# Residual and sums on VectorE in the first layer, a Strassen product for the last features, one finish for the last block

## The chip, the cores and the metric

The kernel runs on one core of a Trainium2 chip. The metric is the time on the device in microseconds (us). PE is TensorE, DVE is VectorE, ACT is ScalarE, POOL is GpSimd, SP is SyncE, whose queue issues every DMA. All data are 32-bit floats.

## The reference

There are two layers over 2048 rows (4 x 512) of width 512. Each norms its input, runs a gated feed-forward product of inner width 1376, norms the result and adds it to the input. In the first, the half of each row of gate values that is smallest by size is set to zero.

```python
def _L0_attn_ref(x, w_gate, w_up, w_down):
    s = jax.nn.silu(jnp.einsum('bsh,ih->bsi', x, w_gate))
    ...
    k = int(K_FACTOR * I)                      # 688 of 1376
    _, idx = jax.lax.top_k(-jnp.abs(s), k)
    ...                                        # flat: s as B*S rows
    flat = flat.at[rows, idx.reshape(B * S, k)].set(0.0)
    s = flat.reshape(B, S, I)
    s = s * jnp.einsum('bsh,ih->bsi', x, w_up)
    return jnp.einsum('bsi,hi->bsh', s, w_down)

def _L0_ffn_ref(x, W_gate, W_up, W_down):
    ...
    y = gate * up @ W_down.T                   # gate = silu(xt @ W_gate.T), up = xt @ W_up.T
    return y.reshape(out_shape)

x = x + _layernorm(_L0_attn_ref(_layernorm(x), ...))
x = x + _layernorm(_L0_ffn_ref(_layernorm(x), ...))
```

## The kernel before

**Products.** Most products are formed as 2x2 block products with seven multiplications instead of eight (Strassen in Winograd's form). The class `Seven` runs one: products p1 to p7 go to three PSUM banks, pa, px and py, and `first`, `second` and `third` evict and add up between them. p7 is accumulated onto px only when px has been added to c12, so a product waits for DVE. `stationary_sums` and `moving_sums` make the sums of the operands on the engine that they are given.

**First layer.** Eight `Unit`s of two 128-row tiles. `norm` norms a tile and transposes it into xT; `products` runs the gate products (pg, L404) in three column pieces, evicts them through ACT, makes the sums S (`sums`, on POOL) and the up products (pau, pxu, pyu, L143). `search` looks for each row's threshold in six steps, each two passes of ACT (L456) and a chain of two- and four-element DVE steps (L461 to L481). `turns` transposes the result (ph, L578; evicted by ACT, L582), `down_sums` makes sums for the down projection on DVE, and `finish` calls `downs`; the difference that p3 needs is made on POOL (L620) after p2. Units are staggered: while unit j multiplies, unit j-1 searches, j-2 is turned and j-3 is finished.

**Second layer.** Four `Block`s of four tiles. `pair` makes gate and up for 2 x 128 features at a time, five times, by `Seven`; `down_sums` makes sums on POOL; `rest` makes the last 96 of the 1376 features by plain products (fg, fu, L681); then `finish` calls `downs` for two pairs of tiles. For the first three blocks both pairs go through one call, and the products of the next block lie between; the last block calls `finish` once for each pair.

**Down projection.** `downs` runs p1, p5, p6 for each pair, then p7, p2, p4, p3. Each product loads 640 KB of weights into a `wd` buffer, of which there are three. `rest` in it adds the last 96 features. `out_norm` norms a tile (bn_stats, bn_aggr, the power -0.5 on POOL at L109, scaling at L114), adds the residual xr on POOL (L331), and stores. With `final` it takes the statistics in halves and adds the residual on DVE (L327, L328).

**Order.** The layers are recorded within a block that a scheduler orders by a simulated timeline, engine by engine; what stands in each queue is its choice. Pools decide when a buffer is free: S, wr and w have one buffer, px, pa and py two banks each. The end of the program loads a flag `badi` on every engine (`values_load`, L875) and branches (L876): a second, general path, `layers("g", True)`, runs only if the threshold search failed somewhere. It does not run in the profiled execution. At the start, 18 transposes of the identity run on PE (`warm`).

## Time and profile before

| what | value |
|---|---|
| median of 3 runs | 888.31 us (886.12 to 889.33) |
| the profiled execution, its own time | 887.46 us |
| its span | 885.5 us |
| mean granted clock of PE | 0.993 |
| PE busy | 862.3 us |
| DVE, ACT, POOL busy | 511.8, 300.9, 180.3 us |
| moved by DMA | 117.54 MB |

The profile is of one execution. A matmul of 32-bit floats shows as two records on PE; records overlap, so that a record's duration is longer than the distance to the next. A wait is named by what ended it. The first layer takes about the first half of the span. Windows are us from the span's start.

### The profile page before, as it was taken

To read this page: it belongs to the slowest core of one execution; us is meant where nothing else is said; L and a number is where in the kernel's file an instruction comes from. 1 tells how busy PE (TensorE), PEld (TensorE's weight loads), DVE (VectorE), ACT (ScalarE), POOL (GpSimd) and SP (SyncE) were. 2 spreads that over 40 slices of the span, in tenths; PEclk is the share of its full clock that TensorE was granted. 3 is DMA by queue.
4 is the path that set the end of the run, shared out by engine and by line. 5 is a ranking of instruction groups with operands and counts; after the bars stand their busy time and mean duration, and the time that the engine had idled before them with its cause. 6 is when DMAs were issued, how large, how long until landed. Compare 5 with 4: busy or idle time off the path is not lost. (4 is left out here: it accounts for less than half of the span.)

```text
span 885.5 us, 10211 instructions
## 1 busy us (share of the span) xinstructions
PE 862.3 (97%) x3588; PEld 652.4 (74%) x3588; DVE 511.8 (58%) x1328; ACT 300.9 (34%) x598; POOL 180.3 (20%) x249
## 2 busy tenths in 40 slices
PE   8999999999999899999999999999999999999995
PEld 5656566757667576677788888888788888888784
DVE  4887776775939578766955434554236443444322
ACT  2465575748463757466011111011101112011100
POOL 2120111212212112110433211321203221122221
PEclk9999999999999999999999999999999999999998
DMA  9999413334232343377374003610045002420064
GB/s 317 360 335 345 165 54 119 120 101 143 78 119 98 103 138 102 119 293 262 132 254 150 0 1 113 195 44 0 30 143 167 1 0 65 143 97 1 30 217 156
DMA packets 62924, 117.54 MB, mean 133 GB/s; under 512 B 4816, under 2 KB 36560, under 8 KB 62864
## 3 DMA queue, kind: packets, MB, share of 16 engines
q1 hardware_dynamic: 62864, 116.80, 39.4%
q8 instruction: 30, 0.49, 0.2%
q14 instruction: 30, 0.25, 0.1%
HBM read 97.91 MB, written 18.87 MB: 132 GB/s over the span
## 5 line engine op out<-in xcount | busy, mean ns | idle before, releaser
L456 ACT ACTIVATE ja<-v,cur 128x1376 bf16<-128x1376 f32 x96 | 138.3, 1441 | 76.9 <-DVE cur L481 54.4
L404 PE MATMUL pg<-wg,xT 128*128 128x456 f32 (+1 forms) x384 | 158.0, 559 | 3.4 <-ACT p L408 2.5
L404 PEld LDWEIGHTS pg<-wg,xT 128*128 128x128 f32 x384 | 73.2, 193 | 68.6 <-issue 59.9
L118 POOL TENSOR_TENSOR D<-hTb 128x256 f32<-128x256 f32 x20 | 14.6, 730 | 180.5 <-DVE hTb L672 180.5
L461 DVE TENSOR_SCALAR low<-cur 128x2 int32<-128x2 f32 x48 | 8.7, 181 | 72.0 <-ACT ja L456 72.0
L143 PE MATMUL pau<-wu,xT 128*128 128x344 f32 x128 | 43.6, 452 | 0.0
L143 PE MATMUL pagb<-xTb,wg 128*128 128x256 f32 x160 | 41.4, 379 | 0.0
L143 PE MATMUL paub<-xTb,wu 128*128 128x256 f32 x160 | 41.3, 380 | 0.0
L143 PE MATMUL pxub<-T,wu 128*128 128x256 f32 x160 | 41.2, 380 | 0.0
L143 PE MATMUL pxgb<-T,wg 128*128 128x256 f32 x160 | 41.1, 379 | 0.0
L258 PE MATMUL pad<-wd_p,hT 128*128 128x256 f32 x160 | 39.4, 380 | 1.3 <-DMA wd_p<-in_L_attn_w_down_dram 1.3
L408 ACT ACTIVATE p<-pg 128x456 f32<-128x456 f32 (+1 forms) x48 | 26.0, 544 | 43.1 <-PE pg L404 39.5
L258 PE MATMUL pxdb<-wdb_p,hTb 128*128 128x256 f32 x160 | 36.7, 379 | 2.1 <-DMA wdb_p<-sum_f 2.1
L258 PE MATMUL pxd<-wd_p,hT 128*128 128x256 f32 x160 | 37.2, 380 | 1.5 <-DVE y L293 1.5
L258 PE MATMUL padb<-wdb_p,hTb 128*128 128x256 f32 x160 | 37.1, 379 | 0.9 <-DMA wdb_p<-in_L_ffn_W_down_dram 0.9
L258 PE MATMUL pydb<-wdb_p,D 128*128 128x256 f32 x160 | 37.9, 379 | 0.1
L258 PEld LDWEIGHTS pxd<-wd_p,hT 128*128 128x128 f32 x160 | 30.3, 190 | 7.4 <-DVE y L293 1.7
L258 PEld LDWEIGHTS padb<-wdb_p,hTb 128*128 128x128 f32 x160 | 30.3, 190 | 7.2 <-issue 3.3
L258 PEld LDWEIGHTS pxdb<-wdb_p,hTb 128*128 128x128 f32 x160 | 30.3, 190 | 6.7 <-issue 2.5
L258 PEld LDWEIGHTS pad<-wd_p,hT 128*128 128x128 f32 x160 | 29.6, 190 | 7.4 <-DMA wd_p<-in_L_attn_w_down_dram 1.7
L258 PEld LDWEIGHTS pydb<-wdb_p,D 128*128 128x128 f32 x160 | 30.1, 190 | 6.2 <-issue 2.5
L670 ACT ACTIVATE sg<-sg 128x768 f32<-128x768 f32 x20 | 16.9, 843 | 50.9 <-DVE sg L167 50.9
(221 smaller groups left out, 1721.9 us busy)
## 6 DMA issues: line engine op xcount, KB each, us to landing
wd_p<-sum_a SPq DMA_DIRECT2D x28, 640.0 KB, 4.0
wd_p<-in_L_attn_w_down_dram SPq DMA_DIRECT2D x21, 640.0 KB, 4.2
wdb_p<-sum_f SPq DMA_DIRECT2D x20, 640.0 KB, 4.1
wdb_p<-in_L_ffn_W_down_dram SPq DMA_DIRECT2D x15, 640.0 KB, 4.2
xn<-in_x_dram SPq DMA_DIRECT2D x16, 256.0 KB, 3.1
xr<-in_x_dram SPq DMA_DIRECT2D x16, 256.0 KB, 2.8
x<-y SPq DMA_DIRECT2D x16, 256.0 KB, 2.0
xnb<-x SPq DMA_DIRECT2D x16, 256.0 KB, 3.1
```

Source lines behind the costliest of these rows:

```text
L118: eng.tensor_add(s1, a21, a22)
L143: nc.tensor.matmul(ps, self.left[k][:, c, :], self.right[k][:, c, :], start=first and c == 0, stop=c == 1, skip_group_check=not first,)
L258: nc.tensor.matmul(p[which], p[1](k, c), ws[k][:, c, :], start=first and c == 0, stop=c == HC - 1, skip_group_check=not first,)
L404: nc.tensor.matmul(pg, self.xT[:, i, c, :], wg[:, c, c0:c1], start=(c == 0), stop=(c == NH - 1),)
L408: nc.scalar.activation(p[:, c0:c1], pg, AF.Silu)
L456: nc.scalar.activation(junk, v, AF.Sign, bias=cur[:, 0, i : i + 1], accum_out=cur[:, 1, i : i + 1],)
L461: nc.vector.tensor_scalar(low, cur[:, 1, :], 0.0, None, ALU.is_gt)
L670: nc.scalar.activation(sg[:, 1:, :], sg[:, 1:, :], AF.Silu)
```

## The change

- `Unit.sums` and the difference for p3 in the first layer are made by DVE instead of POOL.
- `out_norm` has three forms: for the first layer (`dst is x1`) the mean is subtracted and the residual added in one more DVE step; in the second layer it is as before, but for the very last tile, which is normed straight from PSUM (`pa`).
- In the turns of the last but one unit, DVE evicts every second tile instead of ACT.
- `Block.rest` becomes one product by `Seven`: gate and up stand as the two block rows, so its stationary sums are made once, on DVE, ahead of the blocks.
- In `downs` the addition of px to y moves from p2 to p7. The last block finishes both pairs in one call, in the order p7, p3, then p4 and p2 of the first pair, p4 and p2 of the second.
- At the start the first piece of wg is loaded ahead of the second x tile, and six transposes of the first normed tile are added.
- `values_load` and the branch are now within the scheduled block.

```diff
@@ -95,12 +95,13 @@
     def bank(tag, nm):
         return psum.tile([P, 512], F32, tag=tag, name=nm)
 
-    def moments(src, nm, kind, n=1):
-
+    def moments(parts, nm, kind):
+
+        n = len(parts)
         bufs = 1 if kind == "f" else 5
         st = small.tile([P, n, 6], F32, tag="st" + kind, name=f"st_{nm}", bufs=bufs)
-        for i in range(n):
-            nc.vector.bn_stats(st[:, i, :], src[:, ts(i, H // n)])
+        for i in reversed(range(n)):
+            nc.vector.bn_stats(st[:, i, :], parts[i])
         mv = small.tile([P, 2], F32, tag="mv" + kind, name=f"mv_{nm}", bufs=bufs)
         nc.vector.bn_aggr(mv, st)
         ve = small.tile([P, 1], F32, tag="ve" + kind, name=f"ve_{nm}", bufs=bufs)
@@ -110,7 +111,7 @@
         return mv, rs
 
     def layernorm(dst, src, nm, kind):
-        mv, rs = moments(src, nm, kind)
+        mv, rs = moments([src], nm, kind)
         nc.vector.tensor_scalar(dst, src, mv[:, 0:1], rs, ALU.subtract, ALU.mult)
 
     def stationary_sums(eng, a11, a12, a21, a22, s1, s2, s4):
@@ -135,8 +136,8 @@
         def __init__(self, nm, left, right, c12, c21, c22):
             self.left, self.right = left, right
             self.c12, self.c21, self.c22 = c12, c21, c22
-            n = c12.shape[-1]
-            self.pa, self.px, self.py = [bank(k, f"{k}{nm}")[:, :n] for k in ("pa", "px", "py")]
+            m, n = c12.shape
+            self.pa, self.px, self.py = [bank(k, f"{k}{nm}")[:m, :n] for k in ("pa", "px", "py")]
 
         def product(self, ps, k, first=False):
             for c in range(2):
...
@@ -248,12 +250,12 @@
             ]
             st.append((tiles, left, last, pa, px, py, ya, yb))
 
-        def product(k, which, i=None):
+        def product(k, which, i=None, part=slice(None)):
 
             if k not in ws:
                 ws[k] = down_right(work, key, k, w_d, f"{nm}_{pairs[0][0][0]}")
             first = i is not None
-            for p in [st[i]] if first else st:
+            for p in [st[i]] if first else st[part]:
                 for c in range(HC):
                     nc.tensor.matmul(
                         p[which], p[1](k, c), ws[k][:, c, :],
@@ -282,48 +284,78 @@
         def p7():
             product("p7", PX)
             for p in st:
+                tiles, left, last, pa, px, py, ya, yb = p
+                nc.vector.tensor_add(yb[:, hi], yb[:, lo], px)
                 pz.append(bank("pt", f"pz{nm}_{p[0][0]}")[:, :H2])
                 rest(pz[-1], p, 1, hi, True)
 
-        def p2():
-            product("p2", PA)
+        def c22():
             for p, z in zip(st, pz):
                 tiles, left, last, pa, px, py, ya, yb = p
-                rest(pa, p, 0, lo)
-                nc.vector.tensor_add(yb[:, hi], yb[:, lo], px)
                 nc.vector.tensor_add(yb[:, hi], yb[:, hi], py)
                 nc.vector.tensor_add(yb[:, hi], yb[:, hi], z)
-                nc.scalar.copy(ya[:, lo], pa)
-
-        def p4():
-            product("p4", PX)
-            for p in st:
+
+        def p2(part=slice(None)):
+            product("p2", PA, None, part)
+            for p in st[part]:
+                tiles, left, last, pa, px, py, ya, yb = p
+                rest(pa, p, 0, lo)
+                if not final:
+                    nc.scalar.copy(ya[:, lo], pa)
+            if not final:
+                c22()
+            else:
+                for p in st[part]:
+                    tiles, left, last, pa, px, py, ya, yb = p
+                    if p is st[-1]:
+                        out_norm(work, tiles[0], ya, res, dst, nm, pa)
+                    else:
+                        nc.scalar.copy(ya[:, lo], pa)
+                        out_norm(work, tiles[0], ya, res, dst, nm)
+
+        def p4(part=slice(None)):
+            product("p4", PX, None, part)
+            for p in st[part]:
                 tiles, left, last, pa, px, py, ya, yb = p
                 rest(px, p, 1, lo)
                 nc.vector.tensor_add(yb[:, lo], yb[:, lo], px)
                 out_norm(work, tiles[1], yb, res, dst, nm)
 
-        def p3():
-            product("p3", PY)
-            for p in st:
+        def p3(part=slice(None)):
+            product("p3", PY, None, part)
+            for p in st[part]:
                 tiles, left, last, pa, px, py, ya, yb = p
                 rest(py, p, 0, hi)
                 nc.vector.tensor_add(ya[:, hi], ya[:, hi], py)
-                out_norm(work, tiles[0], ya, res, dst, nm, final)
+                if not final:
+                    out_norm(work, tiles[0], ya, res, dst, nm)
 
         heads = [
             f
             for i in range(len(pairs))
             for f in (lambda i=i: p1(i), lambda i=i: product("p5", PY, i), lambda i=i: p6(i))
         ]
-        return heads + [p7, p2, p4, p3]
-
-    def out_norm(work, t, y, res, dst, nm, final=False):
+        if not final:
+            return heads + [p7, p2, p4, p3]
+
+        ends = [lambda f=f, i=i: f(slice(i, i + 1)) for i in range(len(pairs)) for f in (p4, p2)]
+        return heads + [p7, c22, p3] + ends
+
+    def out_norm(work, t, y, res, dst, nm, pa=None):
+
 
         xr = work.tile([P, H], F32, tag="xr", name=f"xr{nm}_{t}")
         nc.sync.dma_start(xr, res[ts(t, P), :])
-        if final:
-            mv, rs = moments(y, f"o{nm}_{t}", "f", 2)
+        if pa is not None:
+            parts = [pa, y[:, H2:]]
+            mv, rs = moments(parts, f"o{nm}_{t}", "f")
+            for i in range(2):
+                nc.vector.tensor_scalar(
+                    y[:, ts(i, H2)], parts[i], mv[:, 0:1], None, ALU.subtract
+                )
+            nc.vector.scalar_tensor_tensor(y, y, rs, xr, ALU.mult, ALU.add)
+        elif dst is x1:
+            mv, rs = moments([y], f"o{nm}_{t}", "o")
             nc.vector.tensor_scalar(y, y, mv[:, 0:1], None, ALU.subtract)
             nc.vector.scalar_tensor_tensor(y, y, rs, xr, ALU.mult, ALU.add)
         else:
@@ -375,7 +407,7 @@
             s = self.work.tile([P, 3, 2, P], F32, tag="S", name=f"S{self.nm}_{self.j}", bufs=1)
             a, b = self.xT[:, 0], self.xT[:, 1]
             self.left = stationary_sums(
-                nc.gpsimd, a[:, :2], a[:, 2:], b[:, :2], b[:, 2:], s[:, 0], s[:, 1], s[:, 2]
+                nc.vector, a[:, :2], a[:, 2:], b[:, :2], b[:, 2:], s[:, 0], s[:, 1], s[:, 2]
             )
 
         def products(self, wg, right, gate_fill, up_fill):
@@ -579,9 +611,10 @@
                         pt[: isz[i], c, :], h[:, i * P : i * P + isz[i]], ident
                     )
                 nf = n if g0 + n <= FULL else n - 1
-                nc.scalar.copy(hT[:, g0 : g0 + nf, :], pt[:, :nf, :])
+                copy = nc.vector.tensor_copy if other and k else nc.scalar.copy
+                copy(hT[:, g0 : g0 + nf, :], pt[:, :nf, :])
                 if nf < n:
-                    nc.scalar.copy(end, pt[: isz[-1], nf, :])
+                    copy(end, pt[: isz[-1], nf, :])
 
             return [lambda k=k, g0=g0: turn(k, g0) for k in range(2) for g0 in range(0, NI, 4)]
 
@@ -617,7 +650,7 @@
             steps[-3]()
             for u in units:
                 a12, s2 = u.dleft["p3"], u.dleft["p6"]
-                nc.gpsimd.tensor_sub(a12, a12, s2)
+                nc.vector.tensor_sub(a12, a12, s2)
 
         return steps[:-3] + [p2] + steps[-2:]
 
@@ -671,20 +704,21 @@
             ms[1].third()
             nc.vector.tensor_mul(h[:, 1:, :], sg[:, 1:, :], h[:, 1:, :])
 
-        def rest(self, wg, wu):
+        def rest(self, left):
 
             n = I - 2 * HF
             nm = f"{self.nm}_{self.b}"
-            pg, pu = bank("pa", f"fg{nm}"), bank("px", f"fu{nm}")
-            for ps, w in ((pg, wg), (pu, wu)):
-                for c in range(NH):
-                    nc.tensor.matmul(
-                        ps[:n, :], w[:, c, 2 * HF :], self.xT[c // 2][:, c % 2, :],
-                        start=(c == 0), stop=(c == NH - 1),
-                    )
+            t = self.work.tile([P, 4, N2], F32, tag="w", name=f"sgr{nm}", bufs=1)[:n]
+            m = Seven(f"rb{nm}", left, self.right, t[:, 0, :], t[:, 1, :], t[:, 2, :])
+            m.first()
+            c11 = m.second()
             h = self.big.tile([P, N], F32, tag="b5", name=f"hTb{nm}_r")
-            nc.scalar.activation(h[:n, :], pg[:n, :], AF.Silu)
-            nc.vector.tensor_mul(h[:n, :], h[:n, :], pu[:n, :])
+            lo, hi = h[:n, :N2], h[:n, N2:]
+            nc.scalar.activation(lo, c11, AF.Silu)
+            m.third()
+            nc.scalar.activation(hi, m.c12, AF.Silu)
+            nc.vector.tensor_mul(lo, lo, m.c21)
+            nc.vector.tensor_mul(hi, hi, m.c22)
             self.h.append(h)
 
         def down_sums(self, c):
@@ -742,8 +776,12 @@
             units = [Unit(j, nm, big, work) for j in range(NU)]
             units[0].load(0)
             units[0].norm(0)
+            if not general:
+                for i in range(6):
+                    nc.tensor.transpose(warm[:, i % 4, :], units[0].x[0][:, :P], ident)
+            wg = load_weight(wpool, a_wg, "wg", f"1{nm}", CH[:1])
             units[0].load(1)
-            wg = load_weight(wpool, a_wg, "wg", f"1{nm}", CH)
+            load_weight(wpool, a_wg, wg, f"1{nm}", CH[1:])
             units[1].load(0)
             units[1].load(1)
             wu = load_weight(
@@ -853,28 +891,31 @@
                 for f in finish([units[-1]], wr):
                     f()
             wr = last_rows(f_wd, 2)
+            t = work.tile([P, 3, 2, I - 2 * HF], F32, tag="S", name=f"wrs{nm}", bufs=1)
+            rest = stationary_sums(
+                nc.vector,
+                *[w[:, 2 * c : 2 * c + 2, 2 * HF :] for w in ws for c in range(2)],
+                t[:, 0], t[:, 1], t[:, 2],
+            )
             for b, block in enumerate(blocks):
                 last = b + 1 == len(blocks)
                 for a in range(HC):
                     block.pair(a, lefts)
                     block.down_sums(a)
-                block.rest(*ws)
-                if last:
-                    block.finish([0], wr)
-                    block.finish([1], wr, True)
-                else:
+                block.rest(rest)
+                if not last:
                     for k in range(TB):
                         blocks[b + 1].norm(k)
                     blocks[b + 1].sums()
-                    block.finish([0, 1], wr)
+                block.finish([0, 1], wr, last)
 
         return badi
 
     with tc.block(schedule_with_timeline_sim=True):
         badi = layers("", False)
-    nbad = nc.values_load(badi[0:1, 0:1], min_val=0, max_val=2 * P * NTT)
-    with tc.If(nbad > 0):
-        layers("g", True)
+        nbad = nc.values_load(badi[0:1, 0:1], min_val=0, max_val=2 * P * NTT)
+        with tc.If(nbad > 0, label="general"):
+            layers("g", True)
 
 
 # ---- launch: one core; inputs and outputs as the reference has them ----
```

## The prediction

> **What bounds the kernel now.** I read the page's busy shares and slices first, then the list of waits of PE, then windows cut on the clock's own borders, then the timeline around each wait of PE.
>
> ```profile
> PE 862.3 (97%) x3588; PEld 652.4 (74%) x3588; DVE 511.8 (58%) x1328; ACT 300.9 (34%) x598; POOL 180.3 (20%) x249
> DVE  4887776775939578766955434554236443444322
> PEclk9999999999999999999999999999999999999998
> ```
>
> PE is busy for 862.3 of 885.5 us. Time can come only from fewer columns streamed through PE, from its 23 us of idle time, or from stretches at half clock. DVE is half empty in the second layer (right half of its digits) and well filled in the first.
>
> ```profile
> PE pg L404 <- ACT p L408: 2.5, 1, 2.5
> PE pxdb L258 <- DMA wdb_p<-sum_f: 2.1, 1, 2.1
> PE pxd L258 <- DVE y L293: 1.5, 1, 1.5
> PE ph L578 <- ACT hT L582: 1.4, 2, 1.1
> PE pad L258 <- DMA wd_p<-in_L_attn_w_down_dram: 1.3, 1, 1.3
> PE padb L258 <- DMA wdb_p<-in_L_ffn_W_down_dram: 0.9, 1, 0.9
> ```
>
> The waits are few and single: two belong to the last block's weight loads (wdb_p), the rest to the first layer and the passage to the second.
>
> ```profile
> 5.30:8.70 3.40, 1.69 (x12) 1.03 (x10) 1.09 (x2) 1.29 (x4) 1.28 (x3) 1.00 1.03 388
> 8.70:12.10 3.40, 3.40 (x5) 1.66 (x6) 0.00 (x0) 0.00 (x0) 1.95 (x3) 0.50 1.04 400
> 295.40:298.80 3.40, 1.24 (x3) 0.68 (x4) 0.58 (x2) 3.27 (x5) 0.55 (x1) 1.00 0.00 0
> 298.80:302.20 3.40, 3.40 (x6) 1.62 (x5) 3.10 (x10) 2.24 (x9) 0.10 (x1) 0.51 0.00 0
> 862.05:865.47 3.42, 2.13 (x10) 1.52 (x8) 0.42 (x1) 0.00 (x0) 0.01 (x1) 1.00 0.93 272
> ```
>
> Columns after the length: busy us of PE, PEld, DVE, ACT, POOL, then the granted clock. A stretch of 3.4 us in which PE is busy for 1.69 or 1.24 us is followed by one at half clock; 2.13 us (third kind) is not punished: the clock stayed at 1.00 behind it. Half clock over 3.4 us costs 1.7 us, twice in this execution.
>
> ```profile
> 285.57 1.27 POOL L331 TENSOR_TENSOR y<-y,xr 128x512 f32<-128x512 f32 x1 [2.10 <-issue]
> 285.77 1.08 DVE L477 SCALAR_TENSOR_TENSOR r<-r,d 128x2 f32<-128x2 f32 x1
> 295.53 1.44 ACT L456 ACTIVATE ja<-v,cur 128x1376 bf16<-128x1376 f32 x1 [3.20 <-DVE cur L481]
> 297.56 2.99 PE L404 MATMUL pg<-wg,xT 128*128 128x464 f32 x5 [2.48 <-ACT p L408]
> ```
>
> A two-element DVE step of the threshold search, 0.15 us elsewhere, takes 1.08 us and ends with POOL's addition. The search is late, ACT stands in line for `cur`, the eviction of pg stands behind it, PE waits 2.48 us and then runs at half clock.
>
> ```profile
> 866.33 2.40 PE L258 MATMUL pxdb<-wdb_p,hTb 128*128 128x256 f32 x10 [2.15 <-DMA wdb_p<-sum_f]
> 876.22 0.60 PE L264 MATMUL pydb<-wr,hTb_r 96*128 96x256 f32 x2
> 876.79 1.26 POOL L331 TENSOR_TENSOR yb<-yb,xrb 128x512 f32<-128x512 f32 x1 [0.66 <-DVE yb L114]
> 879.00 0.75 DVE L328 SCALAR_TENSOR_TENSOR yb<-yb,rs_ob,xrb 128x512 f32<-128x512 f32 x1 [0.44 <-POOL rs_ob L109]
> ...
> L875 SPq TENSOR_LOAD <-badi x1: 520/520/520, 880.2 to 880.2; - x1
> L876 SPq COMPARE_BRANCH  x1: 45/45/45, 881.1 to 881.1; - x1
> L876 SPq EVENT_SEMAPHORE  x8: 17/17/17, 883.6 to 884.2; - x8
> ```
>
> PE ends at 876.82 (call it T). The last DVE step starts at T+2.18, SP issues the store until 880.15, loads badi, branches at 881.1 and goes on at 883.6: 8.7 us without PE.
>
> **The change part by part.** The profiled execution took 887.46 us (span 885.5), 0.85 below the median 888.31 of the runs; the sum is made against 887.46.
>
> *The last 96 features (`Block.rest`).* Pace first: four 512-column records take 1.88 us, of which one is 0.592 long, so 0.429 each; ten 256-column ones take 2.32 with 0.379, so 0.216. Before: 64 records of fg and fu over 4 blocks, 16 x 0.429 = 6.86 us a block. After: 7 products x 2 halves x 2 records = 28 x 0.216 = 6.04. Weight loads of 96 columns take 0.163, under the pace. Gain 0.82 x 4 = 3.3 us. The new evictions (DVE about 2.2 us more a block) fall where DVE is at 4 tenths; the new dependences (p7 behind an addition to px) lie, in the built order, behind 6 or more matmuls of 0.43 us of the following down projection. Its own preparation is four DVE sums, about 1.2 us, at the passage.
>
> *One finish for both pairs of the last block.* Seven loads of 640 KB fewer, and each serves twice the matmuls. Before, PE's waits there are 0.94, 2.15 and 0.45 us, with the restart (0.1 each) 3.7. After, with three wd buffers: p7's load starts when p1 is through and has 14 matmuls of 0.43 us or more, 6.0 us, against 4.1 to land. p3's and p4's start together when p5 is through; p4 is wanted 12 matmuls (5.2 us) later, but lands second: 4.2 us plus 655 KB at the 400 GB/s of the window rows (1.6) is 5.8. I charge 0.8 us of new waiting (bounds 0 and 1.5). Net -2.9.
>
> *The end.* In the built order p4 and p2 of pair 1 come last. p2's own chain loses the addition to y (0.46 us with its gap). But p4's chain (addition 0.42, statistics 0.69, 0.18, 0.15, rs 0.55, scaling 0.55, with gaps 2.8) must fit into p2's 2.6 us, and starts late behind pair 0's: it ends near T+0.4. Then POOL adds its residual for 1.27 us, and the last rs (0.55) is queued behind that addition: about T+1.7 to T+2.3, final step at T+2.35 instead of 2.18. The last xr load is queued on SP behind a store that waits for POOL and lands near T+2.3: no better. Against it, SP's badi load and check stand far ahead in the queue, so its branch follows the store at once: 881.1-880.15 = 0.95 us, capped by the landing of the store and by DVE, which left its branch at 882.8: I take 0.9. Net -0.7. At its new place the badi load waits for a DVE step that precedes by several matmuls those that the loads queued behind it wait for: priced at nothing; its cover is that wait for PE; without it every us would delay a down weight of the last unit.
>
> *The start.* wg's first piece is issued ahead of the second x tile: 256 KB less before it, 0.7 us at 388 GB/s, and PE's 0.92 us wait before 8.63 was on it: -0.7 (xT allows no more). The second x tile lands later, at about 8.5, and is normed under four matmuls. The six added transposes fill that hole. *The rule weighed here:* the Trainium skill ("TensorE: Matmul & The Clock Gate", Part 4: PE-mode transpose) says that transposes do not count as PE activity for the clock; by it the six are worth nothing. The rows speak otherwise: up to 5.3 us PE had run only transposes (18, at half pace), and from 5.30 the clock is 1.00. With them the stretch 5.3 to 8.7 has about 0.3+1.2+0.8 = 2.3 us of PE work, above the unpunished 2.13. By the rows -1.7 us, by the rule 0; I take the rows, and keep 0 for the range since the stretches need not lie alike in every execution.
>
> *First layer: work from POOL to DVE.* Onto DVE: 32 sums of 128x256 (from the 128x512 row 0.684 and the 128x688 row 0.87: 0.41 each) 13.1; 8 differences of 128x640 at 0.82, 6.6; 16 residuals, each 0.48 (L327) + 0.75 (L328) for 0.55 (L114), 11.0; some turned tiles copied, 1.9: 33 us. Off POOL: 29.1 (S sums) + 12.3 (L620) + 20.4 (L331) = 62 us. POOL and DVE hold each other up, as the timeline shows (1.08 for 0.15 above). Means beside the undisturbed lines of the timeline: L463 226 ns against 170 (48 of them), L470 215 against 160, L477 205 and L473 203 against 150 (40 each), L513 389 against 150 (8), L491 1703 against 1650 (16): about 12 us of DVE's time is such waiting. So DVE's net is about +21 us on some 320 busy in 440. DVE at 80% does not bound by itself; the cover is PE's backlog. What the lock caused, the 2.48 us wait with its 1.7 us of half clock and the 1.5 us on y L293 (a 0.55 us scaling took 1.75 there), can go: 5.7 us. The y addition also moves from p2 to p7. Bounds: -8, every such wait gone, to +5, new waits on a fuller in-order DVE, among them residual steps that wait for xr or rs with the search queued behind. I take -2.0. The ACT wait (1.4) and the wd_p wait (1.3) stay: loads and order there are the same.
>
> Sum: -3.3 -2.9 -0.7 -0.7 -1.7 -2.0 = -11.3: 876.2 for a like execution, 877.0 beside the median.
>
> **The rivals.** *Only the certain parts:* the clock gives nothing at the start and the first layer nets to nothing or +2: -7.6 to -5.6, 881 to 883. For it: scheduling against a model leaves a few waits in any order. *All locks gone:* -8 in the first layer, 871. *Slower: DVE becomes the bound of the first layer.* Place: search and passage, where DVE is 19.89 us busy of 20 (420 to 440) and gets some 5 us more. Price: each us of the 33 that PE's backlog doesn't cover. 11 us uncovered undo the gain, 16 make it slower by 0.5%; half uncovered gives 893. Against it: before, PE waited only about 2.5 us for DVE in that layer. *It doesn't do what it says:* the six transposes may end before the hole does, or p4's load be late by more; both are inside the first rival.
>
> **How the numbers follow.** Forecast 874 to 880: 0.50. Certain parts only: 0.27. All locks gone: 0.08. DVE bound: 0.15, half of it slower. A change of about 0.5% (4.4 us) can be told from none here. Faster by more: 0.50+0.08, 0.22 of the second, 0.03 of the last = 0.83; within: 0.10; slower: 0.07. The range 870.5 to 884 leaves out the DVE case and the edges.
>
> **What would show it.** Right: two 256-column record groups in place of fg and fu; no wait of PE on wdb_p over 1 us; PEclk 1.00 from 8.7 us on; SP's branch within 0.1 us of the last store; fewer search steps over 0.5 us. Wrong: PE waits for DVE by more than 10 us before 450 us, or a clock still at 0.50 after the start; a final DVE step later than T+3 would make the end a loss.

## The result, and the profile after

The changed kernel takes 874.58 us (median of 6 runs, 872.70 to 877.11) against 887.16 us of the kernel before beside it (6 runs, 885.12 to 889.33): ratio 0.9863, 95% interval 0.9846 to 0.9880. The forecast was 877.0 (870.5 to 884.0). The profiled execution of after took 873.69 us with a span of 871.9: 13.8 us less than the one of before, where the sum had 11.3.

The page of after, busy times and two rows of the slices:

```profile
PE 855.0 (98%) x3642; PEld 659.8 (76%) x3642; DVE 526.8 (60%) x1417; ACT 302.8 (35%) x601; POOL 117.7 (14%) x193
DVE  5887787776939587667956444454346442444424
PEclk9999999999999999999999999999999999999998
```

PE is busy 7.3 us less, and idle 6.3 us less; it fills 98% of the span. DVE's digits in the first layer are hardly higher than before, although POOL has lost 62.6 us. The clock's digits are 9 up to the last slice.

PE's waits (total, times, longest):

```profile
PE pxub L144 <- DVE hTb L160: 1.8, 1, 1.8
PE ptb L376 <- DVE badi L889: 0.9, 1, 0.9
PE pad L260 <- DMA wd_p<-in_L_attn_w_down_dram: 0.9, 1, 0.9
PE pxu L144 <- DVE c L154: 0.9, 1, 0.9
PE ph L610 <- ACT xTb L378: 0.3, 1, 0.3
```

No wait on wdb_p is left, none on y and none of weight on ACT's p. The two longest that are new (hTb, badi) lie in the passage to the second layer.

The windows at the start and around the longest wait (length; busy us of PE, PEld, DVE, ACT, POOL; granted clock; share and rate of DMA):

```profile
3.40:6.82 3.42, 3.26 (x16) 2.86 (x15) 1.58 (x4) 0.00 (x0) 0.55 (x1) 1.00 1.03 389
6.82:10.23 3.41, 3.41 (x15) 2.06 (x14) 1.58 (x4) 0.65 (x2) 0.55 (x1) 1.00 1.05 397
...
467.62:471.03 3.41, 1.58 (x8) 1.08 (x7) 1.53 (x5) 0.37 (x1) 0.31 (x1) 1.00 0.08 31
471.03:474.44 3.41, 3.41 (x18) 2.93 (x16) 2.14 (x4) 0.00 (x0) 0.23 (x1) 1.00 0.00 0
```

In the stretch ahead of pg's first product PE is busy for 3.26 of 3.42 us, and no half clock follows. (The 1.00 of this first row is no reading. The transposes in it start 0.21 us apart up to 6.67 us and 0.11 us apart from 6.86 on: the clock was at half until about 6.82, where the trace's first record of it begins.) At 467.62 PE is busy for only 1.58 of 3.41 us, and yet the clock stays at 1.00; more on that below.

The wait on hTb, from the timeline:

```profile
465.17 0.40 SPq L368 DMA_DIRECT2D xnb<-x  x1
469.11 0.69 DVE L104 BATCH_NORM_STATS2 st_ib<-xnb 128x6 f32<-128x512 f32 x1 [4.24 <-DMA xnb<-x]
469.72 0.40 DVE L160 TENSOR_TENSOR hTb<-hTb,pxub 128x256 f32<-128x256 f32 x1
470.17 1.13 PE L144 MATMUL pxub<-T,wu 128*128 128x256 f32 x4 [1.83 <-DVE hTb L160]
```

The statistics of a tile of the third block (st_ib) stand on DVE ahead of the step that PE needs (L160). DVE waits 4.24 us for the tile's load, issued at 465.17 and landed at 469.08, and PE waits 1.83 us for DVE.

The search steps on DVE, in groups; first two of before, then the same two of after:

```profile
L463 DVE COPY_PREDICATED lo<-low,cur 128x4 f32<-128x4 int32 x48 | 10.9, 226 | 1.0
L477 DVE SCALAR_TENSOR_TENSOR r<-r,d 128x2 f32<-128x2 f32 x40 | 8.2, 205 | 0.9
...
L495 DVE COPY_PREDICATED lo<-low,cur 128x4 f32<-128x4 int32 x48 | 7.7, 160 | 0.8
L509 DVE SCALAR_TENSOR_TENSOR r<-r,d 128x2 f32<-128x2 f32 x40 | 6.2, 155 | 0.8
```

L495 is L463 of before, and L509 is L477, which was 205 ns in the mean and took 1080 ns in one instance, at 285.77 us. Now they run at 155 to 160 ns. DVE's busy time up to the flag's matmul is 328.2 us for 325.2, although POOL's there fell from 84.1 to 25.1.

The end, from the timeline of DVE, POOL and SP; then the rows of the branch by its source line (DVE and SP: branch, and the semaphore instructions behind it, with first and last start):

```profile
859.41 0.42 SPq L348 DMA_DIRECT2D xrb<-x  x1
...
862.21 0.55 DVE L115 TENSOR_SCALAR yb<-yb,mv_ob,rs_ob 128x512 f32<-128x512 f32 x1 [0.66 <-POOL rs_ob L110]
863.83 1.43 DVE L353 TENSOR_SCALAR yb<-yb,mv_ob 128x256 f32<-128x256 f32 x1
863.85 1.26 POOL L363 TENSOR_TENSOR yb<-yb,xrb 128x512 f32<-128x512 f32 x1 [1.68 <-DMA xrb<-x]
865.07 0.60 POOL L110 TENSOR_TENSOR rs_ob<-ve_ob,nhalf 128x1 f32<-128x1 f32 x1
865.13 1.68 SPq L364 DMA_DIRECT2D out_dram<-yb  x2
865.70 0.75 DVE L356 SCALAR_TENSOR_TENSOR yb<-yb,rs_ob,xrb 128x512 f32<-128x512 f32 x1 [0.44 <-POOL rs_ob L110]
```

```profile
L917 DVEq COMPARE_BRANCH  x1: 76/76/76, 866.6 to 866.6; - x1
L917 SPq COMPARE_BRANCH  x1: 45/45/45, 866.9 to 866.9; - x1
L917 DVEq EVENT_SEMAPHORE  x1: 21/21/21, 870.3 to 870.3; - x1
L917 SPq EVENT_SEMAPHORE  x8: 17/17/17, 870.0 to 870.5; - x8
```

PE's last product ends at T = 862.42. POOL waits 1.68 us for the xrb issued at 859.41, adds for 1.26 us, and only then makes the last rs. DVE's subtraction beside that addition takes 1.43 us (0.34 in e8, where no addition runs beside it). The last DVE step starts at T + 3.28; before it was T + 2.18.

Where the 13.6 us of span went, by marks that every kernel here has: the flag's matmul (pbad), the first pagb product of the second block, the first product of the last block's last 96 features, PE's end, the span's end. All times in us; the medians were each taken beside runs of the kernel before, whose median was 885.8 to 887.7.

| kernel | start to flag | to second block | to last block's last features | to PE's end | to span's end | median, ratio to before (interval) |
|---|---|---|---|---|---|---|
| before | 448.24 | 118.06 | 262.46 | 48.05 | 8.69 | |
| after | 437.48 | 120.47 | 261.11 | 43.35 | 9.49 | 874.58, 0.9863 (0.9846 to 0.9880) |
| e1, three moves undone | 447.64 | 119.46 | 261.17 | 43.46 | 11.67 | 886.73, 1.0002 (0.9989 to 1.0015) |
| e2, before with the moves | 439.04 | 122.93 | 262.98 | 48.10 | 9.05 | 882.46, 0.9952 (0.9936 to 0.9968) |
| e3, no transposes | 436.13 | 123.77 | 261.10 | 43.56 | 9.63 | 875.41, 0.9869 (0.9845 to 0.9892) |
| e4, end and ACT's queue | 438.10 | 118.91 | 261.15 | 43.67 | 8.27 | 872.91, 0.9850 (0.9827 to 0.9873) |
| e5, residual on POOL | 440.22 | 118.15 | 261.19 | 43.35 | 10.59 | 877.64, 0.9903 (0.9884 to 0.9922) |
| e6, plain features | 436.39 | 123.41 | 262.46 | 44.18 | 10.66 | 876.58, 0.9886 (0.9868 to 0.9904) |
| e7, two finishes | 436.27 | 121.97 | 261.23 | 46.89 | 8.35 | 876.85, 0.9899 (0.9881 to 0.9916) |
| e8, end and c buffers | 436.29 | 119.80 | 261.13 | 43.35 | 8.43 | 870.43, 0.9818 (0.9804 to 0.9833) |
| e9, e8 and flag on ACT | 438.41 | 118.39 | 261.50 | 43.75 | 8.25 | 873.08, 0.9844 (0.9816 to 0.9872) |
| e10, before with the start | 453.60 | 118.08 | 262.46 | 47.80 | 8.86 | 892.34, 1.0065 (1.0042 to 1.0087) |
| e11, flag's load outside | 436.31 | 121.08 | 261.21 | 43.35 | 12.35 | 876.28, 0.9886 (0.9857 to 0.9916) |
| e12, e2 and the start | 438.89 | 122.08 | 262.46 | 48.11 | 8.96 | 882.35, 0.9944 (0.9924 to 0.9965) |

Half clock is in these figures, 1.7 us for each stretch: two in before's first column, two in e3's second and one in that of e2, e6, e7, e8, e11 and e12; after has none from 6.82 us on. So 3.4 of the 10.8 us that after gains up to the flag are half clock of the one execution of before. After and e8, whose products stand in the same order up to the flag, differ by 1.2 us there: less than that can't be read from one trace.

From before to after: -10.8 to the flag, +2.4 in the passage, -1.35 and -4.7 in the rest of the second layer, +0.8 at the end.

### The profile page after: what moved, and what is told of

The parts are those of the page before. It is cut to its first block, busy times and chain, and to the rows that moved or that the text cites. A ratio compares the mean times of both kernels' runs of the same rounds, so it can differ in the third digit from the quotient of the medians.

```text
span 871.9 us, 10340 instructions
## 1 busy us (share of the span) xinstructions
PE 855.0 (98%) x3642; PEld 659.8 (76%) x3642; DVE 526.8 (60%) x1417; ACT 302.8 (35%) x601; POOL 117.7 (14%) x193
## 5 line engine op out<-in xcount | busy, mean ns | idle before, releaser
L436 PE MATMUL pg<-wg,xT 128*128 128x456 f32 (+1 forms) x384 | 154.8, 549 | 0.2 <-ACT p L440 0.2
L119 POOL TENSOR_TENSOR D<-hTb 128x256 f32<-128x256 f32 x20 | 14.6, 729 | 169.7 <-DVE hTb L705 169.7
L110 POOL TENSOR_TENSOR rs_o<-ve_o,nhalf 128x1 f32<-128x1 f32 x16 | 11.6, 724 | 188.6 <-DVE ve_o L108 188.5
L144 PEld LDWEIGHTS pxub<-T,wu 128*128 128x128 f32 x160 | 30.1, 190 | 6.9 <-DVE hTb L160 2.2
```

The lines of the kernel that those rows point to most:

```text
L110: nc.gpsimd.tensor_tensor(rs, ve, nhalf, ALU.pow)
L119: eng.tensor_add(s1, a21, a22)
L144: nc.tensor.matmul(ps, self.left[k][:, c, :], self.right[k][:, c, :], start=first and c == 0, stop=c == 1, skip_group_check=not first,)
L436: nc.tensor.matmul(pg, self.xT[:, i, c, :], wg[:, c, c0:c1], start=(c == 0), stop=(c == NH - 1),)
```

## The experiments

**e1: the three moves undone.**

```diff
-                nc.vector, a[:, :2], a[:, 2:], b[:, :2], b[:, 2:], s[:, 0], s[:, 1], s[:, 2]
+                nc.gpsimd, a[:, :2], a[:, 2:], b[:, :2], b[:, 2:], s[:, 0], s[:, 1], s[:, 2]
...
-                nc.vector.tensor_sub(a12, a12, s2)
+                nc.gpsimd.tensor_sub(a12, a12, s2)
...
-        elif dst is x1:
+        elif False:
```

> The changed kernel, but in the first layer the residual addition, the sums S and the fourth down operand's difference are made by POOL again; all else stays as changed. Theory A (locks): what the first layer gained came from taking POOL's work out of DVE's way. Then DVE steps over their undisturbed length come back (19.5 us before the flag's matmul in the kernel before, 0.0 in the changed one), PE waits on ACT or DVE again before 450 us, and the run is 4 to 6 us longer than the changed kernel (875): 879 to 881. Rival B (order): the gain came from the earlier addition of px, the turned tiles on DVE and the luck of the schedule; then the time stays within 1.5 us of 875 though the long DVE steps are back. In both the wait of PE on hTb at the passage (2.2 us of distance) should shrink if the residual on DVE causes it, and stay if the late load of xnb alone does.

886.73 us: the whole gain is gone, twice what theory A had asked for. 10.2 us of it are lost ahead of the flag. One of the waits, from the timeline of e1:

```profile
351.81 0.72 POOL L119 TENSOR_TENSOR S<-xT 128x256 f32<-128x256 f32 x1 [4.52 <-issue]
351.90 0.65 DVE L505 SCALAR_TENSOR_TENSOR r<-lo,r 128x2 f32<-128x2 f32 x1
352.61 0.73 POOL L120 TENSOR_TENSOR S<-S,xT 128x256 f32<-128x256 f32 x1
352.78 0.57 DVE L513 TENSOR_TENSOR cur<-lo,r 128x2 f32<-128x2 f32 x1
353.41 0.73 POOL L122 TENSOR_TENSOR S<-xT,S 128x256 f32<-128x256 f32 x1
353.45 1.44 ACT L488 ACTIVATE ja<-v,cur 128x1376 bf16<-128x1376 f32 x1 [1.77 <-DVE cur L513]
...
354.89 0.54 ACT L440 ACTIVATE p<-pg 128x464 f32<-128x464 f32 x1
...
355.48 1.04 PE L436 MATMUL pg<-wg,xT 128*128 128x464 f32 x2 [1.52 <-ACT p L440]
```

POOL's sums S (L119, L120, L122) run beside two search steps of two elements, which take 0.65 and 0.57 us for the usual 0.16 (the Trainium skill, "SBUF — State Buffer", section "Who interferes with whom", has DVE and GpSimd share a pair of ports under an exclusive lock; these rows agree); ACT stands idle 1.77 us ahead of the search's pass, 0.9 of which are what the two steps took too long; the eviction of pg stands behind it, and PE waits 1.52 us. A gap beyond PE's pace is the distance between the starts of two records less the usual one for their shape. Between 100 us and the flag e1 has 11 gaps of over 0.3 us beyond the pace (behind ACT's p, c, xT, he and hT, and DVE's c, D, ve_o and y), 11.1 us in all, where after has two, 0.8 us: the difference is about the 10.2 us. DVE steps that run longer than their kind usually does add up to 21.6 us ahead of 450 us in e1, 32 steps, each beside an instruction of POOL, and to none in after. The chain is that of the prediction, its size is not. But the scheduler orders each kernel anew (one in six of PE's records up to the flag stands elsewhere in e1), and how much of the 10.2 us is the new order and how much the stretched steps is not shown. The wait on hTb in the passage is gone in e1, the one on badi (1.7 us) is there.

**e2: the three moves alone, on the kernel before.** The same three edits.

> The kernel before, with nothing changed but these three moves from POOL to DVE in the first layer. Theory A (locks): 4 to 6 us shorter than the kernel before (887): 881 to 883; the flag's matmul comes about 7 us earlier, the passage costs some 2 to 3 us of it. Rival B (order): 885 to 889, no difference to be told. Rival C, the one of the prediction that ends slower (DVE as the bound): over 889.

882.46 us, 3.6 less than before (886.01). The flag comes 9.2 us earlier, 3.4 of which are the two stretches at half clock of the trace before that this one does not have. The passage then takes 4.9 us more than before. The waits of e2, and the windows at its passage:

```profile
PE pxub L143 <- DVE hTb L159: 1.9, 1, 1.9
PE pz L264 <- DVE badi L855: 1.8, 1, 1.8
```

```profile
468.80:472.21 3.41, 1.55 (x8) 1.05 (x6) 1.53 (x5) 0.37 (x1) 0.00 (x0) 1.00 0.22 83
472.21:475.62 3.41, 3.41 (x10) 2.69 (x9) 0.91 (x2) 0.00 (x0) 0.55 (x1) 0.50 0.00 0
...
4.59:8.00 3.41, 1.97 (x14) 1.29 (x12) 1.83 (x7) 0.74 (x3) 1.17 (x2) 1.00 0.93 306
8.00:11.41 3.41, 2.54 (x7) 1.37 (x8) 1.27 (x3) 0.56 (x2) 0.00 (x0) 1.00 1.03 395
```

1.9 and 1.8 us of waits stand where before had none, and the one on hTb is followed by 3.4 us at half clock (1.7 us). So the moves are worth 5.8 us up to the flag here, with the half clock of before taken out, and 10.2 in e1, where neither trace has any; what is left of it at the end depends on the passage.

**e3: without the six transposes.**

```diff
             if not general:
-                for i in range(6):
-                    nc.tensor.transpose(warm[:, i % 4, :], units[0].x[0][:, :P], ident)
+                pass
```

> The changed kernel without the six added transposes at the start; the order of the loads stays. By the rows of the trace of before (a stretch with little PE work is followed by one at half clock): the hole of 0.8 us ahead of 7.5 us comes back, and one stretch of 3.4 us is granted half clock: +1.7 us against the changed kernel, and the clock of the first 14 us shows 0.50 once. If the six only fill a hole that the clock does not punish: within 0.3 us, clock 1.00 throughout. By the rule that transposes do not count for the clock: 0 as well.

875.41 us, no difference from after that can be told. pg starts at 7.51 us as in after, the clock is full from 6.99 us to 440 us, and the flag is even earlier. So the six are worth nothing that can be told, and the 1.7 us that were expected of the rows did not come. The clock of this execution does fall twice in the passage, which after's did not:

```profile
467.79:471.20 3.41, 1.38 (x7) 0.88 (x7) 1.53 (x5) 0.37 (x1) 0.21 (x1) 1.00 0.02 9
471.20:474.61 3.41, 3.41 (x10) 2.69 (x9) 0.88 (x2) 0.00 (x0) 0.34 (x1) 0.50 0.00 0
437.07:440.48 3.41, 1.70 (x9) 1.01 (x9) 3.02 (x10) 0.00 (x0) 0.77 (x2) 1.00 0.96 314
440.48:443.89 3.41, 3.41 (x9) 2.70 (x9) 1.80 (x3) 0.00 (x0) 1.01 (x1) 0.50 0.82 301
```

From the product ahead of the wait on hTb to the next are 2.4 us here, and 2.2 in after, with the clock's borders at 467.79 instead of 467.62.

**e4: the end and the passage mended, first try.** Within the last block the residual tiles of the last pair are loaded at c22 into xn buffers, the last residual but one is added by DVE, and xn of the second layer is loaded through ACT's queue.

```diff
+            if final:
+                for t in st[-1][0]:
+                    xrs[t] = residual(work, t, res, nm, "xn", bufs=3)
...
-        elif dst is x1:
+        elif dst is x1 or dve:
...
-            normed_T(load_x(self.work, x1, t, nm), t, dsts, nm)
+            normed_T(load_x(self.work, x1, t, nm, eng=nc.scalar), t, dsts, nm)
```

> The changed kernel with two mends. At the end: the last pair's residual tiles are loaded when p7 is through, into the free xn buffers, and the last residual but one is added by DVE instead of POOL, so that nothing stands on POOL ahead of the last rs. At the passage: the second layer's input tiles are loaded through ACT's queue instead of SP's, so that they do not stand behind stores that wait for a residual. If the end is as read in the trace (POOL waits 1.68 us for xrb, adds for 1.26, the last rs stands behind it), the last DVE step starts at PE's end + 2.4 instead of + 3.28: -0.9 us. If the wait on hTb comes from xnb standing behind a store, it goes: -2 us more, 872 in all. Rival: ACT's own queue holds the loads as long, or ACT is held by them: the passage stays at its 2.2 us or grows.

872.91 us. The end took 8.27 us for 9.49, as expected. In the passage this wait of PE fell from 1.8 to 1.1 us and did not go: through ACT's queue the load is issued at 464.32 for 465.17, so SP's queue was not all that held it: the transposes that free an xn buffer start at 463.80 and take 0.49 us.

**e5: only the residual back on POOL.**

```diff
-        elif dst is x1:
+        elif False:
```

> The changed kernel, but in the first layer only the residual addition is back on POOL; the sums S and the difference stay on DVE. With all three back on POOL the flag's matmul came 10.2 us later (447.64 for 437.48). If the harm goes by POOL's time, the residual is 20.4 of its 62 us: a third, flag near 441, and 3 to 4 us longer in all: 878. If the residual is the harmful one (1.27 us long and on the path of a tile's norm, while the sums are four short steps of 0.45 us): most of the 10, 883 or more. If the long POOL chain of the sums S is the one: within 1 us of the changed kernel. For the passage: from the flag to the second block the changed kernel takes 120.5 us, 2.4 more than the kernel before although its last features are 0.8 shorter; if the residual step on DVE causes that, it falls to 118; if the early statistics of xnb do, it stays at 120.

877.64 us, 3.1 above after. The flag is 2.7 us later, a quarter of e1's 10.2, so that sums S and the difference have by far the most (7.4, by the difference between the two runs; it was not run alone). In e5 ten DVE steps are stretched, by 8.7 us, and PE's gaps up to the flag are 3.2 us. The passage is 2.3 us shorter than after's: with the residual on POOL the order there is another, and the wait on hTb is not there.

**e6: the last 96 features by plain products.** `rest` and its call as in the kernel before.

```diff
-                block.rest(rest)
+                block.rest(*ws)
```

> The changed kernel, but with the last 96 features by plain products as in the kernel before. By the pace of records: +0.82 us a block, +3.3 in all (878), of it +2.5 between the second block's first product and PE's end (304.5 in the changed kernel), and no new wait. Rival: the dependences of the seven products cost part of it, and the plain form loses less than 2 us.

876.58 us, 2.0 above after, with intervals that overlap. The trace tells more: from the second block's first product to PE's end 306.64 for 304.46, 2.2 us for three blocks instead of the 2.5 of the sum. The end is longer in e6 as the last xrb landed late:

```profile
871.00 0.75 DVE L356 SCALAR_TENSOR_TENSOR yb<-yb,rs_ob,xrb 128x512 f32<-128x512 f32 x1 [2.83 <-DMA xrb<-x]
```

**e7: the last block in two calls.**

```diff
-                block.finish([0, 1], wr, last)
+                if last:
+                    block.finish([0], wr)
+                    block.finish([1], wr, True)
+                else:
+                    block.finish([0, 1], wr)
```

> The changed kernel, but the last block finishes its two pairs of tiles in two calls, so that each of the seven weights is loaded twice. By the waits of the kernel before: +3.7 us of PE's waits on wdb_p, in two or three waits of 0.5 to 2.2 us, from the last features of the last block to PE's end (43.35 us in the changed kernel, so 47). Rival: the new order of products (p3 ahead of p4 and p2) asks for the loads early enough, and it costs under 1 us. The end after PE's last record may move by half a us either way.

876.85 us. To PE's end 46.89 us for 43.35: +3.5. The waits are back on the doubled loads, and one on DVE's turn at the bank:

```profile
PE pxdb L260 <- DMA wdb_p<-sum_f: 1.5, 2, 1.2
PE pydb L260 <- DVE yb L295: 1.0, 1, 1.0
```

**e8: the end mended, and other buffers at the passage.** The end as in e4, loads on SP, and

```diff
-            normed_T(load_x(self.work, x1, t, nm), t, dsts, nm)
+            kw = dict(tag="c", bufs=2) if self.b > 1 else {}
+            normed_T(load_x(self.work, x1, t, nm, **kw), t, dsts, nm)
```

> The changed kernel with the end mended as before (the last pair's residual tiles loaded when p7 is through, the last residual but one on DVE), and the loads left on SP's queue; at the passage the third and fourth blocks' input tiles use the buffers of c, which the second layer leaves free. The load of the third block's first tile at 465 us waits for an xn buffer (freed by the transposes that end at 464.0), and its statistics stand on DVE ahead of the step that PE waits for. If that buffer is the cause, the wait on hTb at 468 to 470 goes: -2 us, and with the end -3, 871.5. Rival: the statistics, standing earlier on DVE, wait for the same 4 us load at an earlier place and hold other steps: no gain at the passage or a loss of up to 3 us.

870.43 us, ratio 0.9818 (0.9804 to 0.9833): faster than both kernels, 4.1 us below after. The wait on hTb is gone and the end takes 8.43 us:

```profile
PE ptb L388 <- DVE badi L902: 1.7, 1, 1.7
PE pad L260 <- DMA wd_p<-in_L_attn_w_down_dram: 0.3, 1, 0.3
```

```profile
862.14 0.61 POOL L110 TENSOR_TENSOR rs_ob<-ve_ob,nhalf 128x1 f32<-128x1 f32 x1 [1.64 <-DVE ve_ob L108]
862.82 0.75 DVE L368 SCALAR_TENSOR_TENSOR yb<-yb,rs_ob,xrb 128x512 f32<-128x512 f32 x1
```

The last rs follows its ve at once, and the last DVE step starts 2.25 us after PE's end (860.57) instead of 3.28. The 1.7 us for badi that are left are followed by a stretch at half clock in this execution.

**e9: e8, and the flag evicted by ACT.**

```diff
-                nc.vector.tensor_copy(badi, pb[:1, :1])
+                nc.scalar.copy(badi, pb[:1, :1])
```

> The last one (end mended, third and fourth block's input tiles in the buffers of c) with one more edit: the flag badi is evicted by ACT instead of DVE. In that one PE waits 1.9 us at 438 us for the bank of pbad, because DVE's eviction stands behind statistics that wait for a load of xnb, and the stretch after it is granted half clock (440.9). If that is the cause, the wait goes, and with it 1.7 us of half clock wherever the clock's borders had punished it: 2 to 3.5 us less than 870.4, so 867 to 868.5. Rival: PE only waits a little later for the same statistics (the transposes of xnb come next on PE), and nothing or 0.5 us is won.

873.08 us: no better, by the medians worse. The rival held: the wait on badi is gone, and 1.3 us for ve_ib stand in its place. PE also waited in this execution at 36 and 71 us, for the norm of xn and for c, 2.6 us beyond its pace.

**e10: the new start alone, on the kernel before.**

```diff
-            units[0].load(1)
-            wg = load_weight(wpool, a_wg, "wg", f"1{nm}", CH)
+            if not general:
+                for i in range(6):
+                    nc.tensor.transpose(warm[:, i % 4, :], units[0].x[0][:, :P], ident)
+            wg = load_weight(wpool, a_wg, "wg", f"1{nm}", CH[:1])
+            units[0].load(1)
+            load_weight(wpool, a_wg, wg, f"1{nm}", CH[1:])
```

> The kernel before with nothing changed but the start (first piece of wg ahead of the second x tile, six transposes of the first tile). By the traces of the changed kernel, with and without the six: first product of pg at 7.5 us instead of 8.6, -1.1 us. If half clock behind the start is the rule in the kernel before, -1.7 on top, 883.2; if it depends on where the clock's borders fall, as the trace of the three moves alone has it (same start, borders at 4.59 and 8.00, no half clock), -1.1 on the median, 884.8 or no difference to be told.

892.34 us: slower than before, which no theory had. pg starts at 7.03 us and the clock is full from 4.5 us to the end, yet the flag comes at 453.60, 5.4 us later. PE's longest waits:

```profile
PE pxd L258 <- DMA wd_p<-sum_a: 3.3, 1, 3.3
PE pg L404 <- ACT p L408: 2.9, 2, 1.5
```

The order that the scheduler finds with this start is another in the whole first layer, and with POOL's work in it PE waits in many places, 0.5 to 2 us at each and 3.3 us once for wd_p. No half clock is in e10's time to the flag; without the 3.4 us of it in before's, the loss is 8.8 us.

**e11: the flag's load outside the scheduled block.** `values_load` and `If` as in the kernel before.

> The changed kernel, but the flag is loaded behind the scheduled block as in the kernel before. By the prediction SP's load of the flag and its check behind the last store cost 0.9 us: from the last DVE step to the end of the span 7.1 us instead of 6.2. By the two traces (6.5 before, 6.2 after, since SP and DVE leave the branch 3.1 and 3.7 us after it now, 2.5 and 3.1 before) only 0.3: 6.5. At 441 us SP then has no flag to wait for; if the wait for it was hidden, nothing moves there.

876.28 us; the interval (0.9857 to 0.9916) holds after's ratio too. In the trace SP's branch starts 0.96 us after the issue of its last store ends (866.49, 867.45), as the prediction had it; in after it is 0.06 us. From the last DVE step (865.37) to the span's end are 8.9 us, where after has 6.2 and before 6.5. 2.15 us of them are a hole between the second and third of SP's eight semaphore instructions (870.40 to 872.55), for which the trace shows no wait:

```profile
L917 SPq EVENT_SEMAPHORE  x8: 17/17/17, 870.3 to 872.9; - x8
```

The eight take 0.5 us in after and 2.6 here. What the hole is was not settled; without it the load outside costs 0.6 us. At 441 us the flag's load was hidden: the next down load on SP is issued at 443.43 in after, with the flag's load 1.9 us ahead of it, and at 444.69 in e11 without one.

**e12: the moves and the start, on the kernel before.** The edits of e2 and e10.

> The kernel before with the three moves from POOL to DVE and the new start, and nothing else. The start alone made that kernel slower (892.3 for 887.1; the flag's matmul at 453.6 for 448.2), with eight waits of PE of 0.5 to 2 us in the first layer while steps of DVE were stretched by POOL; the moves alone made it faster (882.5; flag 439.0). If the loss with the start was the order and the locks between POOL and DVE, it is gone with the moves: flag at 436 to 437.5, 880 to 881. If the start's own order costs time (the second tile's transposes later, PE ahead of the search), the flag stays at 439 or later and the time at 882 or more. A third, that start and moves add up: flag at 444, 887.

882.35 us, e2's time, and 10 us below e10. The flag is at 438.89 for 439.04 of e2, though pg starts at 7.88 instead of 8.87. Of the three expectations the second is the nearest, at its border: e10's loss is gone, and yet the head start brings nothing that can be told. So the loss went with the order and POOL's work together; the two were not parted.

With e12 the moves stand in three pairs of kernels, each pair with its own other code. Stretched steps are DVE's, ahead of 450 us; gaps are PE's beyond its pace, from 100 us to the flag, without half clock; all in us.

| pair: POOL's work on POOL, on DVE | flag comes earlier by (without half clock) | stretched steps | PE's gaps |
|---|---|---|---|
| before, e2 | 9.2 (5.8) | 19.2, 0 | 7.5, 1.5 |
| e1, after | 10.2 | 21.6, 0 | 11.1, 0.8 |
| e10, e12 | 14.7 | 20.4, 0 | 15.6, 2.8 |

In each pair about one in six of PE's records stands elsewhere. That the moves bring the gain is shown three times; that they do so by the stretched steps alone is not: 4.6 of e10's 15.6 us are waits for wd_p.

## Why the prediction was right, and where it was not

The direction was right and the time is 2.4 us below the one predicted, but the second is partly luck: the terms missed by up to 6.4 us, in both directions. Step by step, in the prediction's own order:

- **The last 96 features, -3.3.** Right. The pace held, no PE wait stands on `rest`, and e6 has 2.2 us for three blocks of 0.82 each.
- **One finish, -2.9.** Right in mechanism; the 0.8 us charged for p4's load were not needed. All 3.7 us of waits are gone, and e7 brings 3.5 back (1.5 on the loads, 1.0 on DVE, and restarts). p4's load landed at 846.41 and its first product started at 846.70.
- **The end, -0.7.** Wrong in sign: +0.8. The step that failed is the final DVE step at T + 2.35; it came at T + 3.28. The prediction had seen POOL's residual ahead of the last rs, but let it start when p4's tile was scaled, near T + 0.4. It started at T + 1.43: the scaling ended at T + 0.34, and the xrb of this tile, loaded behind a store that waits for POOL too, landed at T + 1.27. The prediction had asked when the last xr lands, not the one before it. Its own sign of a loss, a last step later than T + 3, came true. e8 takes both causes away and has the last step at T + 2.25. The other half, SP's branch 0.9 us sooner, was too large as well: it did move up to the last store (866.81 and 866.87), but from the last DVE step to the span's end only 0.3 us were won (6.5 to 6.2; 0.6 by e11), because DVE went on 3.7 us after its branch where it took 3.1 before, and SP 3.1 where it took 2.5.
- **The start, -0.7 and -1.7.** Seen in the trace (pg at 7.51 for 8.63, no half clock), and yet wrong as a gain: e12 against e2 is 0.1 us. PE, earlier by 1 us, waits later: in e12 1.1 us for ACT's hT at 397 us, beyond its pace, where e2 has no gap; in after 0.9 us for DVE at 71 us, and in e9 and e10 1.6 and 1.5 at the same place. As to the rule of the Trainium skill on transposes that was weighed ("TensorE: Matmul & The Clock Gate", Part 4), e2 has the rows for it, and they are against it. Up to 8.00 us PE ran transposes alone; their starts are 0.21 us apart up to 4.54 us and 0.11 from 4.68 on, so the clock became full behind nothing else. From 4.59 to 8.00 there are 1.97 us of them, and the next stretch was granted 1.00. So no half clock followed in e2, although it has the start of before: whether it falls there depends on the execution.
- **First layer, -2.0 (-8 to +5).** Mis-sized. Of the 10.8 us up to the flag 3.4 are half clock (1.7 of them counted under the start), and 7.4 are left. PE's gaps beyond its pace between 100 us and the flag (those over 0.3 us) went from 7.5 to 0.8 us: with the half clock at 298.9 (1.7) this is about the lower bound of the step. The chain named (POOL's step, a late search step, ACT in line, PE waits) is seen in e1. What failed was the price put against it: with 5.7 to 8 us that could go, -2.0 leaves 3.7 to 6 us for new waits on DVE's +21 us of work, and there were almost none in that layer. DVE's busy time up to the flag rose by 3.0 us, and by 12.0 behind it. The wait on ACT's hT (1.4), said to stay, is gone; 0.3 us on ACT's xTb stand there. DVE as the bound, the rival that ended slower, did not occur. The new waits came elsewhere, at +2.4 in the passage (+3.2 without the shorter features), which the sum had at nothing: PE waits there for the step behind the statistics of a tile of the third block, whose load had no buffer until 464 us. With another buffer (e8) that wait is gone.

Sum by place: start and first layer to the flag -10.8 (predicted -4.4), second layer -6.05 from the second block to PE's end (-5.4), passage +2.4 (-0.8), end +0.8 (-0.7). The errors partly cancelled.

## What to carry to other kernels

The delay from POOL's work beside a chain of tiny DVE steps is paid at many places along the chain, most of them short. Add up all gaps of PE in the stage, the short ones too: here nearly the whole sum went (7.5 to 0.8 us, and 11.1 for 0.8 with the moves undone in the finished kernel). Undo a move in the finished kernel as well, as the rest of the code changes what it is worth (5.8, 10.2 and 14.7 us here). A head start at the beginning is worth nothing while a later chain sets the pace (1 us of it was gone by the flag in e12): look for the first wait behind it. In an in-order engine a prefetched tile's first step needs a buffer that is free and a load that has landed, or it holds what PE waits for.

## What the runs showed of the hardware

- Half clock goes by stretches of 3.41 us whose borders lie differently in each execution, so the same wait is punished in one and not in the other: behind 1.55 and 1.70 us of PE work it fell (e2, e3), behind 1.58 (after) and 1.97 (e2) it stayed full. No limit in PE's busy time comes out of these rows, since it fell behind 1.79 us too (e6, 436.25 to 439.66) and stayed full behind 1.57 (e1, 221.73 to 225.14). The Trainium skill ("TensorE: Matmul & The Clock Gate", Part 1) has such a free-running window, but names an idle one as what brings half clock; here stretches with 1.24 to 1.79 us of work brought it. Six runs of e3 show the steps in time: at a mean granted clock of 0.992 they took 876.0 and 877.1 us, at 0.994 874.9 and 876.7, at 0.996 872.4 and 874.0.
- With the order of two loads and six transposes changed, the first layer came out 5.4 us longer (e10) where POOL made the sums beside DVE, and 0.1 shorter where it didn't (e12). In the ten profiled kernels with all three moves the flag lies between 436.1 and 439.0, in the three with none between 447.6 and 453.6.
- Behind the final branch 2.15 us were lost between two instructions of SP that wait for nothing that the trace shows (e11, one execution).
